# Keys and values of two attention layers by seven products of quarters

## The chip, the cores and the metric

The kernel runs on one core of a Trainium2 chip. Times are device microseconds (us) of one execution; 1428.65 us is the median of three runs of the kernel before. The profile is of one further execution. Its engines are named PE (TensorE, with PEld for its weight loads), DVE (VectorE), ACT (ScalarE), POOL (GpSimd) and SP (SyncE, which issues the DMAs here).

## The reference, cut to what matters

`x` is 8 batches of 512 tokens by 512 features, `ctx` 8 batches of 120 tokens by 512. Four stages follow each other, each added to `x` with a gate:

```python
x = x + tanh(g_xattn[0]) * xattn0(layernorm(x), ctx)          # 16 heads of 32
x = x + tanh(g_ffn[0])   * routed_ffn(layernorm(x))           # 128 experts
x = x + tanh(g_xattn[1]) * xattn1(layernorm(x), ctx, mask)    # with biases and a mask
x = x + tanh(g_ffn[1])   * channel_mix(layernorm(x))

# each xattn:
q, k, v = y @ Wq.T (+ bq), ctx @ Wk.T (+ bk), ctx @ Wv.T (+ bv)
out = softmax(q k^T / sqrt(32)) v @ Wo.T (+ bo)
```

The change concerns `k` and `v` of both attention layers: for each, a 960 x 512 matrix (all tokens of the context) times a 512 x 512 matrix. All of it is float32.

## The kernel before, in words

Both attention layers are objects of one class, `CrossAttention`. Its constructor loads, projects the keys and values and brings the first batches of queries on their way; `run` then goes through 32 tiles of 128 tokens, a slot for each, and `tail` ends the layer. In `run` the slot of tile t computes the scores and softmax of tile t+1, two or fewer products of the queries five tiles ahead, the transposes of the probabilities of t, the output of t-1, and normalizes and transposes later tiles of `x`.

**Keys.** `project_keys` (L333 on) works on two halves of the context, four batches or 480 tokens each. In layer 1 the context comes with tokens on partitions and is first transposed on PE, a batch at a time (`turn_context`); the result `ctxT` is stored to a DRAM tensor, `aside`, at the end. In layer 2 it is loaded from there, already turned. For each of four blocks of 128 features, four matmuls (L345) of 480 columns add up one PSUM bank, and ACT moves it to `kT` with the softmax's scale and, in layer 2, the bias.

**Values.** `project_values` (L379) takes one batch: four matmuls of 512 columns, with the context's 120 tokens as the stationary side, then DVE moves the bank to `v`, adding the bias in layer 2. Three of the eight batches come ahead of the first transposes of `x`, three between them, and two behind the first scores.

**Queries** are already computed by seven products of quarters (`SevenProducts`), as is much of the last stage. Both factors are cut into four quarters of 256 x 256; four sums of quarters of each factor are made first (S1 to S4 of the left, T1 to T4 of the right), each from earlier ones, in the order S3, S1, S2, S4 and T3, T1, T2, T4. Then seven products replace eight. They run in the order p1, p2, p6, p5, p7, p4, p3:

- p1 and p2 need no sum of both sides; p6 needs S2 and T2, p5 S1 and T1, p7 S3 and T3, p4 T4, p3 S4.
- ACT moves p1 and p5 out of PSUM, DVE the others, adding to what is there.
- p7 is followed by two additions in SBUF on POOL (L192, L193): the first reads the quarter that p4's instruction on DVE (L198) changes next, the second changes the quarter that p3's (L203) adds to.

A product of four matmuls takes one of the four PSUM banks tagged `mm`, which are shared by everything in the layer but the scores and half of the probabilities' transposes; these have two tiles of two banks (`s`).

**Order.** In the constructors the order of the instructions on every engine, SP among them, is that of the program text (`manual_schedule(engines=every)`). In `run` of layer 1 only PE's order is by hand, in layer 2 PE's and SP's; a planner orders the rest. All DMAs but two small ones are issued by SP, one after the other.

**Statistics.** `stats(t)` is a pair of DVE instructions for one tile of `x`; after each fourth, POOL makes the batch's scales in four small instructions (L58 to L64). All 32 tiles of both layers have theirs in the constructor.

**Memory.** Pools on the right side of SBUF stack down from its end, and a pool's first tile lies lowest. In layer 2 the pool `at_v` comes first: `ctxT` (15,360 bytes a partition) and `bv` (2,048); below it `at_k` with a second copy of the context, `ctx` (15,360), `wk` and the mask's rows. The keys read `ctx` (L285 loads it in two halves), the values `ctxT` (L302). A tile may be written when the tiles that lay there before have had their last reader. In the routed stage before layer 2 the pool at the end of memory holds `permT` (16,384) and then three small tiles (2,208 with padding); its last readers are the last matmuls of the scatter (L1031). Below lie a pool of the routing, `hT` (16,384) and the experts' weights, which are free some 26 us earlier.

## Time and profile before

| what | us |
|---|---|
| median of three runs (1428.62 to 1429.21) | 1428.65 |
| the profiled execution | 1431.72 |
| its span, first to last instruction | 1429.9 |
| PE busy, in the span | 1383.4 |
| layer 1: first matmul of the keys, of the values | 13.27, 41.69 |
| layer 1: first scores, second scores | 79.33, 91.37 |
| layer 2: first matmul of the keys, of the values | 693.25, 719.1 |
| layer 2: second scores (their mask) | 768.91 |

The mean granted TensorE clock of the profiled execution is 0.995. A row of a timeline gives the start and the length in us, the engine, the line of the kernel and what it writes and reads; `xN` says that N instructions are merged. A row by stretches gives the stretch, its length, and for PE, PEld, DVE, ACT and POOL the busy time and the number of instructions, then the granted clock, the busy share of the DMA engines and GB/s. A row of waits reads "who <- for whom: us in all, times, longest". SPq is SP's queue of DMA issues. A group's mean length of a matmul holds its latency as well; the distance between starts is what a train of them costs.

### The profile page before, as it was taken

The page shows a single profiled execution, that of the slowest core. Times are in us where ns is not written, and L with a number is a line of the kernel's source. Part 1 is how long each engine was busy: PE and PEld are TensorE (multiplying, and loading weights), DVE is VectorE, ACT ScalarE, POOL GpSimd, SP SyncE. Part 2 cuts the span into 40 slices and gives each one's busy share as a digit, 9 for nine tenths or more (in the row PEclk, how much of TensorE's full clock was granted, in tenths as well). Part 3 has the DMA queues.
Part 4 walks back from the last instruction along what each step waited for, and adds up shares of the span by engine and source line. Part 5 has one row for each costly group of instructions (what it writes and reads, how often), then busy time and mean ns, then how long its engine had stood idle before and what let it go on. Part 6 is the DMA issues. An engine that isn't in the chain of part 4 may idle for free.

```text
span 1429.9 us, 32488 instructions
## 1 busy us (share of the span) xinstructions
PE 1383.4 (97%) x13696; PEld 1067.2 (75%) x13696; DVE 1020.5 (71%) x1453; ACT 768.2 (54%) x1870; POOL 644.0 (45%) x576
## 2 busy tenths in 40 slices
PE   7999999999999997999999999999998999999997
PEld 3577777777776787888657777777776788888886
DVE  2666777777777676777566777777777588887786
ACT  1256666666666445444225665666566555445543
POOL 1425545545444000555375575565546333343331
PEclk9999999999999999999999999999999999999999
DMA  9400000000001337432501000000000000000001
GB/s 301 162 9 24 24 23 23 24 23 16 24 31 43 131 125 227 133 106 87 173 0 60 2 2 1 2 2 2 2 30 2 1 30 30 30 30 30 30 16 45
DMA packets 45240, 73.39 MB, mean 51 GB/s; under 512 B 2925, under 2 KB 21869, under 8 KB 44837
## 3 DMA queue, kind: packets, MB, share of 16 engines
q1 hardware_dynamic: 44805, 71.30, 15.0%
q8 instruction: 108, 1.77, 0.5%
q14 instruction: 39, 0.32, 0.1%
q10 hardware_dynamic: 288, 0.00, 0.0%
HBM read 52.55 MB, written 18.74 MB: 50 GB/s over the span
## 4 chain that ended last, share of the span: by engine, by line
PE 72%; DVE 14%; ACT 6%; POOL 4%; issue 3%; DMA 1%; POOLq 0%; SPq 0%; DVEq 0%; ACTq 0%
PE ops L616 15%; PE qps L149 13%; PE tps L564 6%; PE cps L149 5%; PE aps L599 5%; PE s L507 4%; PE kps L345 4%; PE rps L1010 3%; PE vps L379 3%; PE l1ps L925 2%; PE rlps L749 2%; PE ops L1031 2%; PE gps L898 2%; PE xnps L439 2%; DVE rT L990 2%
## 5 line engine op out<-in xcount | busy, mean ns | idle before, releaser
L525 POOL TENSOR_TENSOR pr<-pr,rs 128x960 f32<-128x960 f32 x128 | 229.4, 1795 | 253.2 <-DVE rs L524 231.7
L616 PE MATMUL ops<-wo,aT 128*128 128x512 f32 x512 | 240.6, 596 | 0.7 <-ACT aT L607 0.7
L535 ACT ACTIVATE pr<-s,nmx 128x120 f32<-128x120 f32 x512 | 176.8, 371 | 114.0 <-DVE nmx L532 110.1
L616 PEld LDWEIGHTS ops<-wo,aT 128*128 128x128 f32 x512 | 92.6, 191 | 72.5 <-issue 67.8
L1023 POOL TENSOR_TENSOR r<-r,b 128x1024 f32<-128x1024 f32 x31 | 73.5, 2377 | 145.2 <-ACT r L1022 145.2
L149 PE MATMUL qps<-xnT,wq 128*128 128x256 f32 x512 | 119.6, 381 | 0.0
L564 PEld LDWEIGHTS tps<-ident,pr 128*120 128x120 f32 x864 | 96.7, 138 | 29.6 <-issue 26.2
L543 DVE TENSOR_REDUCE mx<-s 128x8 f32<-128x960 f32 x64 | 74.0, 1156 | 56.6 <-PE s L507 56.6
L535 ACT ACTIVATION_READ_ACCUMULATOR pr<-s,nmx 128x1 f32 x512 | 111.1, 217 | 0.0
L564 PE MATMUL tps<-ident,pr 128*120 128x128 f32 x864 | 104.9, 273 | 2.5 <-ACT pr L535 1.3
L149 PEld LDWEIGHTS qps<-xnT,wq 128*128 128x128 f32 x512 | 95.7, 189 | 15.2 <-issue 1.0
L551 DVE TENSOR_REDUCE sm<-pr 128x8 f32<-128x960 f32 x64 | 73.5, 1148 | 21.9 <-ACT pr L546 21.8
L49 DVE BATCH_NORM_STATS2 bnst<-x 128x6 f32<-128x512 f32 x128 | 86.8, 678 | 1.3
L440 ACT COPY xnT<-xnps 128x512 f32<-128x512 f32 x64 | 38.1, 595 | 82.0 <-PE xnps L439 82.0
L532 DVE TENSOR_REDUCE nmx<-s 128x8 f32<-128x960 f32 x64 | 73.5, 1148 | 8.3 <-PE s L507 8.3
L599 PE MATMUL aps<-prT,v 120*32 120x128 f32 x2048 | 73.3, 278 | 4.1 <-ACT prT L589 2.2
L545 DVE TENSOR_TENSOR pr<-s,mx 128x960 f32<-128x960 f32 x64 | 73.5, 1149 | 0.9
L1276 POOL TENSOR_TENSOR x<-x,cv 128x512 f32<-128x512 f32 x28 | 41.5, 1480 | 70.7 <-DVE cv L1273 70.7
L574 ACT COPY prT<-tps 120x1024 f32<-120x1024 f32 x54 | 55.0, 1019 | 32.7 <-PE tps L564 32.7
L507 PE MATMUL s<-kT,qT 32*128 32x120 f32 x2048 | 71.9, 278 | 0.0
L507 PEld LDWEIGHTS s<-kT,qT 32*128 32x128 f32 x2048 | 66.5, 188 | 6.5 <-issue 6.3
L599 PEld LDWEIGHTS aps<-prT,v 120*32 120x32 f32 x2048 | 53.8, 110 | 18.3 <-issue 8.6
(191 smaller groups left out, 3088.2 us busy)
## 6 DMA issues: line engine op xcount, KB each, us to landing
w<-in_w_dram SPq DMA_DIRECT2D x32, 512.0 KB, 4.8
x<-in_x_dram SPq DMA_DIRECT2D x8, 1024.0 KB, 15.4
aside<-x SPq DMA_DIRECT2D x32, 256.0 KB, 2.0
x<-aside SPq DMA_DIRECT2D x8, 1024.0 KB, 10.5
out_dram<-x SPq DMA_DIRECT2D x14, 512.0 KB, 2.8
wk<-in_wk_dram SPq DMA_DIRECT2D x3, 1024.0 KB, 8.8
wv<-in_wv_dram SPq DMA_DIRECT2D x3, 1024.0 KB, 5.6
wq<-in_wq_dram SPq DMA_DIRECT2D x2, 1024.0 KB, 15.7
```

The lines of the kernel that those rows point to most:

```text
L49: cm.nc.vector.bn_stats(st, cm.x[:, t, :])
L149: self.nc.tensor.matmul(ps[:, m, :], self.a[a][:, k, m * P : (m + 1) * P], self.b[b][:, k, :], start=(k == 0), stop=(k == 1),)
L507: nc.tensor.matmul(s[j // 2][:, j % 2, hc * LK : (hc + 1) * LK], self.qT[b][r : r + 32, hc, toks], self.kT[r : r + 32, hc, keys], start=no ...
L525: nc.gpsimd.tensor_tensor(pr[:, js, :, :], pr[:, js, :, :], rs[:, js, :, :].to_broadcast([P, 2, NC, LK]), ALU.mult,)
L532: nc.vector.tensor_reduce(nmx, sv[1], AX.X, ALU.max, negate=True)
L535: nc.scalar.activation(pr[:, 2 + j, hc, :], sv[1][:, j, hc, :], AF.Exp, bias=nmx[:, j, hc, :], accum_out=sm[:, 2 + j, hc : hc + 1],)
L543: nc.vector.tensor_reduce(mx, sv[0], AX.X, ALU.max)
L545: nc.vector.tensor_tensor(pv, sv[0], mx.to_broadcast([P, 2, NC, LK]), ALU.subtract)
L551: nc.vector.tensor_reduce(sm[:, :2, :], pv, AX.X, ALU.add)
L564: nc.tensor.transpose(ps[:, jj, hc * P : (hc + 1) * P], pr[:, 2 * u + jj, hc, :], self.cm.ident,)
L599: nc.tensor.matmul(aps[32 * j : 32 * j + 32, hc, :], self.v[b // 2][:LK, b % 2, h * HD : (h + 1) * HD], prT[:, j, hc, :], start=True, stop ...
L616: nc.tensor.matmul(ops, self.aT[t][:, c, :], self.wo[:, c, :], start=(c == 0), stop=(c == NC - 1),)
```

## The change

Keys and values are computed with `SevenProducts` too, a half of the context at a time. The left factor is the weight, the right one the half's turned context, 480 tokens in two quarters of 240. The context's sums T1 to T4 of a half are made once, on POOL, and serve keys and values. The sums of `wk` are made on DVE, those of `wv` on POOL. For the values the roles on PE are exchanged (`turned=LK`): a quarter of 120 tokens is the stationary side, 256 columns of `wv` move. Each half gives 7 products of 4 matmuls for keys, of 240 columns, and 7 of 4 for values, of 256.

With it come these edits:

- The context is held in two tiles, `ctxT[0]` and `ctxT[1]`, both in `at_v`; layer 2 loads each of them once, and the second copy is gone. The sums (`csums`), a spare quarter and half a bias (`bvmore`) lie in `at_v` as well, the sums of `wk` in `at_k`, those of `wv` in the second buffer of the probabilities.
- Layer 1 stores the context to `aside` in two halves, after the keys.
- All values are computed before the queries, and the first scores come last in the prologue.
- The statistics of tiles 16 to 31 move into the slots of `run`; those of tiles 8 to 15 stand between the products of the values.
- The softmax's scale is taken by the copies of the transposed `x` (and by `bq`) in place of the keys.
- The queries' T3 lies in the tile of `qT` that they will fill, which is therefore taken one step earlier; the tiles `prT` and `aT` come from a pool that is opened after the prologue.

```diff
 def load(self, ins, loads, mask, biases):
-        self.ctxT = vp.tile([P, NC, B * LK], FP, name="ctxT")
+        half, own = B * LK // 2, 3 if self.turned else 4
+        self.ctxT = [vp.tile([P, NC, half], FP, name=f"ctxT{h}") for h in range(2)]
+        self.csums = [vp.tile([P, own, 2, half // 2], FP, name=f"cs{h}") for h in range(2)]
+        self.q5 = vp.tile([P, 2, 256], FP, name="cq5")
...
+            self.bvmore = vp.tile([LK, D // 2], FP, name="bvmore")
+        wks = kp.tile([P, 3, 2, 256], FP, name="wks")
-        if self.turned:
-            self.ctx = kp.tile([P, NC, B * LK], FP, name="ctx")
...
         def half(h):
             if self.turned:
                 keys = slice(h * B * LK // 2, (h + 1) * B * LK // 2)
-                nc.sync.dma_start(out=self.ctx[:, :, keys], in_=self.aside[:, :, keys])
+                nc.sync.dma_start(out=self.ctxT[h], in_=self.aside[:, :, keys])
...
         weights(self.wv, wvT)
-        if self.turned:
-            nc.sync.dma_start(out=self.ctxT, in_=self.aside)
...
+    def sum_context(self, h, engine):
+        n = B * LK // 4
+        if self.turned:
+            sums = [quarter(self.ctxT[h], 0, 1, n)]
+            sums += [self.csums[h][:, i] for i in range(3)]
+        else:
+            sums = [self.csums[h][:, i] for i in range(4)]
+        for step in SevenProducts.right_steps(self.ctxT[h], *sums, engine, n=n):
+            step()
+        return SevenProducts.right(self.ctxT[h], *sums, n=n)
...
+    def project_keys(self):
+        nc = self.nc
+        self.ctx7 = [None, None]
+        if not self.turned:
+            for b in range(4):
+                self.turn_context(b)
+        self.wk7 = self.sum_weights(self.wk, self.wks, nc.vector)
+        self.ctx7[0] = self.sum_context(0, nc.gpsimd)
+        k = self.keys(0)
+        k.next(2)
+        if not self.turned:
+            for b in range(4, B):
+                self.turn_context(b)
+        k.next(2)
+        self.stats_of_batch(0)
+        self.ctx7[1] = self.sum_context(1, nc.gpsimd)
+        k.next(3)
+        if self.biased:
+            nc.gpsimd.tensor_scalar(self.gbo, self.gbo, self.gate, None, ALU.mult)
+        for t in range(2):
+            self.normalize(t)
...
+        k = self.keys(1)
+        k.next(4)
+        self.stats_of_batch(1)
+        self.wv7 = self.sum_weights(self.wv, [self.wvs[:, i] for i in range(3)], nc.gpsimd)
+        k.next(3)
+        if not self.turned:
+            for h in range(2):
+                keys = slice(h * B * LK // 2, (h + 1) * B * LK // 2)
+                nc.sync.dma_start(out=self.aside[:, :, keys], in_=self.ctxT[h])
 
     def prologue(self):
-        for b in range(3):
-            self.project_values(b)
-        for t in range(2 * TB):
+        nc = self.nc
+        self.sum_query_weights()
+        v = self.values(0)
+        for n in range(7):
+            v.next()
+            if n < 4:
+                self.stats(2 * TB + n)
+        v = self.values(1)
+        for t in range(TB):
+            v.next()
             self.transpose_x(t)
             self.normalize(t + 2)
-            if t < TB - 1:
-                self.project_values(t + 3)
-            elif t < 2 * TB - 1:
-                self.queries(0, t + 1 - TB)
-        rest = self.scores(0)
-        for b in range(B - 2, B):
-            self.project_values(b)
-        rest()
+            self.stats(3 * TB + t)
+        v.next(3)
+        for f in range(NC):
+            self.queries(0, f)
+            self.transpose_x(TB + f)
+            self.normalize(TB + f + 2)
+        self.scores(0)()
...
     def transpose_x(self, t):
-        nc.scalar.copy(self.xnT[b][:, :, i * P : (i + 1) * P], ps)
+        dst = self.xnT[b][:, :, i * P : (i + 1) * P]
+        nc.scalar.activation(dst, ps, AF.Copy, scale=SM_SCALE)
...
     def run(self):
         for t in range(-1, NT - TB - 1):
+            if 4 * TB <= t + 14 < NT:
+                self.stats(t + 14)
```

## The prediction

> **What bounds the kernel now.** I read, in this order: the busy shares of the page, the busy time by stretch, the spacing of the instructions of the two projections and of what the change puts in their place, and the queue of SP with the landings. TensorE first:

> ```profile
> PE 1383.4 (97%) x13696; PEld 1067.2 (75%) x13696; DVE 1020.5 (71%) x1453; ACT 768.2 (54%) x1870; POOL 644.0 (45%) x576
> ```

> By stretch (length, then busy time and instructions of PE, weight loads, DVE, ACT, POOL; granted clock; DMA). The four are keys and the rest up to the first scores in layer 1, then in layer 2:

> ```profile
> 13.30:41.70 28.40, 27.75 (x81) 13.87 (x82) 10.46 (x26) 5.12 (x9) 9.09 (x14) 1.00 1.05 367
> 41.70:93.00 51.30, 50.19 (x239) 31.29 (x238) 35.45 (x68) 18.91 (x41) 15.79 (x27) 1.00 0.19 74
> 693.00:719.00 26.00, 26.00 (x72) 12.26 (x66) 10.59 (x27) 4.63 (x7) 3.58 (x7) 1.00 0.65 229
> 719.00:766.00 47.00, 45.88 (x194) 27.54 (x193) 32.33 (x65) 17.52 (x39) 34.10 (x45) 1.00 0.00 1
> ```

> PE is the bound in all four; nothing else is late by more than 1.1 us. So fewer columns through PE are worth their full time, as long as the other queues keep up. Prices, as the timeline has them (start, length, engine and line):

> ```profile
> 13.27 13.15 PE L345 MATMUL kps<-ctxT,wk 128*128 128x480 f32 x32 [0.65 <-ACT ctxT L371]
> 41.69 10.46 PE L379 MATMUL vps<-wv,ctxT 128*120 128x512 f32 x24
> 64.04 3.62 PE L149 MATMUL qps<-xnT,wq 128*128 128x256 f32 x16
> 33.56 1.27 POOL L88 TENSOR_TENSOR wqs<-wq 128x512 f32<-128x512 f32 x1
> 65.58 0.69 DVE L107 TENSOR_TENSOR xnT<-xnT 128x512 f32<-128x512 f32 x1
> ```

> Every call of matmul stands as two instructions. A long train ends some 0.2 us after its last start, so 32 in 12.9 are 0.403 us each, 24 in 10.3 are 0.429, and 16 in 3.46 are 0.216: in proportion to the columns.

> **The products.** Keys, per layer: 64 x 0.403 = 25.8 us go. In their place come 2 halves x 7 products x 8 instructions of 240 columns; 0.216 x 240/256 = 0.202, so 1.61 a product and 22.6 in all. (From 0.190, the length of a weight load, to 0.216: 1.3 less to 1.6 more.) Values: 64 x 0.429 = 27.5 go, 14 products of 8 x 0.216 = 1.73 come, 24.2. PE has 6.5 us less to do in each layer, 13.1 in both.

> **What comes for it on the other queues.** Per layer POOL gets 8 additions for the sums of the context (128x480), 4 for those of wv, and two after each of four p7. Rows of such additions on POOL run from 1.09 (xns) to 1.59 (kT of the last stage), most at 1.27. I take 1.27 for 512 columns from a weight, 1.27 x 480/512 = 1.2 for the rest: 24 us, in a stretch in which POOL works 9.1 + 15.8 us in layer 1. DVE gets 4 x 0.69 for wk, ahead of need. Each p7, p4 and p3 is now tied to POOL: p4 writes where the first of p7's additions on POOL still reads, and p3 adds to what the second makes. The queries show that wait already:

> ```profile
> DVE qT L198 <- POOL qT L192: 21.4, 16, 1.4
> ```

> There POOL is free when p7 comes. In the change it isn't: in program order p7 of a half stands behind normalization scales and the four sums of the next operand. While p4 and p3 wait, they hold two of the four PSUM banks, and DVE's queue stands still behind p4's instruction, p2 and p6 of the next set among it.

> **Layer 1, queue by queue.** p1 and p2 of the first half need no sums and run from 13.3 to 16.5. The second half of the context landed 15.5 us after its issue at 1.71, so at 17.2: a wait of 0.7 (the old first half hid it). The transposes and the other five products end at 27.1, p1 and p2 of the second half at 30.3. POOL meanwhile: x of batch 0 lands 19.3 us after 3.11, at 22.4; four statistics at 0.80 make 25.6; scales (four small instructions, 1.97) 27.6; three of the context sums 31.2, where p6 gets its operand (1.0 waited); the fourth 32.4, p7's two until 34.7. p5 waits for the bank of p4 (1.5). Keys end at 40.9, before at 41.7. The same again: statistics 40.0, scales 42.1, sums of wv 43.3 to 47.1, p7's two 49.4; p6 of the values waits 1.6 for the third sum and p5 1.4 for a bank. Values end at 70.3 with four transposes of x among them, queries and four more at 85.3, and scores(0) starts at 85.8, when the last addition is in.
> What goes with the order: the old scores(0), at 79.3, had 7.1 us of values behind it while its softmax held the score banks for 5.95 us. Now only 3.9 us (two query products, a transpose) stand there, so scores(1) starts at 85.8 + 6.05 = 91.9, before at 91.4. **Layer 1: +0.5 us**; the 6.5 are gone. With additions at 1.02 and 1.09 it is -0.9, at 1.49 and 1.59 it is +3.0.

> **Layer 2: a load that moves.** The old kernel loads the context twice. SP's queue, and one of its waits (who, for what, us, times, longest):

> ```profile
> 667.29 0.63 SPq L285 DMA_DIRECT2D ctx<-turned  x1
> 667.97 0.61 SPq L291 DMA_DIRECT2D wk<-in_wk_dram  x1
> 668.62 0.53 SPq L285 DMA_DIRECT2D ctx<-turned  x1
> 690.75 0.34 SPq L299 DMA_DIRECT2D bqk<-in_bqk_dram  x1
> 691.21 0.37 SPq L291 DMA_DIRECT2D wv<-in_wv_dram  x1
> 693.31 0.34 SPq L302 DMA_DIRECT2D ctxT<-turned  x1
> ```
> ```profile
> SPq L302 <- PE ops L1031: 1.7, 1, 1.7
> ```

> The keys' copy lay in at_k, over memory that the experts freed at 667. The other lay in at_v, at the end of memory, over permT, which the last scatter of layer 1 reads until 693.3. The change drops the first and keeps only the one in at_v. The tiles there now make 32,000 bytes a partition: ctxT0 lies 24,320 to 32,000 from the end, ctxT1 16,640 to 24,320, and permT 2,208 to 18,592. So ctxT0 still loads at 667, but ctxT1 overlaps permT by 1,952 bytes, waits until 693.3, and bqk, wv and all later loads stand behind it on SP. A half alone lands in

> ```profile
> ctx<-turned SPq DMA_DIRECT2D x1, 960.0 KB, 5.3
> ```

> so at 698.6. bqk, behind it, I put at 699.0 (bv, behind the old ctxT, landed 0.9 after it); were it not held by the data ahead, its own 2.0 us would make 696. Without bqk POOL's first instruction, scale_biases, can't run, and the context's sums are queued behind that. POOL: 699.0 + 0.45 + 3 x 1.2 = 703.1. PE has done p1 and p2 by 696.5 and **waits 6.6 us** for p6. From there as in layer 1, with 1.5 more for a bank; keys end at 724.1 (before 719.1). Then POOL has gbo (1.58), two additions to x (1.26), scales, the wv sums and p7's two until 733.1. Here p1 of the values goes out on DVE too, behind p4 and p3 of the keys, so no bank at all comes free before 732.7: **5.2 us**. Values end at 755.3, scores(0) starts at 770.9, scores(1) at 771 + 6.3 = 777.2; before 768.9. **Layer 2: +8.3** (with bqk at 696, +5.3; additions at the low and high rows, +6.3 and +11.6).

> **What PE does after a gap.** After 9.16 us without work the sixteen transposes of the context took 3.43 us, the next sixteen 1.80, both at a granted clock of 1.00:

> ```profile
> 9.19 3.43 PE L366 MATMUL ctps<-ident,ctx 120*128 120x120 f32 x16 [9.19 <-DMA ctx<-in_ctx_dram]
> 26.25 1.80 PE L366 MATMUL ctps<-ident,ctx 120*128 120x120 f32 x16
> ```

> So 1.6 us are lost behind a gap of 9.2, and none is seen behind one of 2.6 (at 537.6). 6.6 is nearer to the first, 5.2 to the second: I take **+1.6** for the one and 0 for the other (0 to 3.3 in all).
> [...]

> **Edits that I cost at nothing.** Sixteen statistics a layer (0.84 on DVE each, scales on POOL every fourth slot) move from the prologue into the slots of run. DVE waits there for the scores once a slot, which is what hides them:

> ```profile
> DVE mx L543 <- PE s L507: 32.0, 26, 2.2
> ```

> That is 1.2 us each; were the cover gone, up to 13 us a layer, but DVE is busy 224 of 312 us there and PE waits for it next to never, so 0 to +1. The second load of 1,920 KB goes: its reader started at 719, it landed at 703; 0. The store to aside becomes two after the keys; SP has nothing behind it until 87.6, and the reader is layer 2. Scaling moves from the keys to the transposes' copies: ACT took 0.57 with a scale and 0.56 to 0.59 without. T3 goes into the tile of qT one slot earlier; its last reader, scores(t+1), stands ahead on PE. prT and aT start in memory that the values freed one stage earlier.

> **Sum.** -13.1 (PE's work) and +23.5 of new waits and lost cover: 0.5 + 8.3 + 1.6 = +10.4. The profiled execution took 1431.72 us (span 1429.9 and 1.8 around it), so 1442.1; it stood 3.07 above the median of the runs, 1428.65, and against that I say 1439.0.

> **Rivals.** (B) ctxT1 doesn't wait, since memory is laid out otherwise than I add it up. Then bqk lands at 692.8 as before, p6 waits 0.2 instead of 6.6, the gap's price goes: layer 2 +2.2, sum +2.7, 1431.3. For it: my layout is only added up from sizes. Against it: the old ctxT did wait for that scatter. (C) The other side: POOL's queue isn't in the way, because its additions are over before PE comes to them. With them at nothing, layer 1 gives -5.5 and layer 2, which keeps the load's wait, -2.2: 1421. The sign turns where an addition takes about 0.75 us (1.2 gives +8.8, 0.69 gives -1.4, both without the gap's price); the cheapest row is 1.09, which speaks against it. (D) Additions at the dear rows, 1.49 and 1.59: +14.6 without the gap's price, 1443 to 1446. That 240 columns cost no less than 256 would move the sum by 0.2 only, since PE then waits less.

> **How the numbers follow.** My forecast 0.62 (its own range 1434 to 1443), B 0.20 (1428 to 1434), C 0.10 (1418 to 1428), D 0.08. A measurement of this kernel tells 0.2%, 2.9 us, from nothing: 1425.8 to 1431.5 is the same. B lies half in it: faster 0.10, same 0.11, slower 0.79. The range from 1430 to 1445 leaves out C, a third of B and some of D.

> **What would show it.** Right: SP's second load of layer 2 at 693.3, waiting for ops; a PE gap of 6 to 7 us ahead of the third product of the keys, ended by POOL, and one of about 5 in the values; in layer 1 scores(1) within 2 us of 91.4; fewer matmul columns, and a lower busy share of PE. Wrong: that load at 668.6; PE without gaps between 16 and 60; POOL additions far from 1.2; PE waiting on DVE in the slots of run.

## The result, and the profile after

The changed kernel takes 1450.71 us (median, 1449.55 to 1451.50), the kernel before 1428.93 on the same chip: a ratio of 1.0145, 95% interval 1.0125 to 1.0165 (estimated from all runs; it need not be the quotient of the medians). It is 1.45% slower. The forecast was 1439.0, with a range from 1430 to 1445: the sign is right, the loss twice as large as forecast (10.4). The profiled execution took 1450.38 us, its span 1448.6, against 1431.72 and 1429.9 before: +18.7 us to be found in the traces.

The busy line of TensorE and the others after:

```profile
PE 1377.3 (95%) x13888; PEld 1108.0 (76%) x13888; DVE 1040.1 (72%) x1492; ACT 765.3 (53%) x1870; POOL 692.0 (48%) x616
```

TensorE works less, as intended, but only by 6.1 us, and its share falls from 97 to 95%. The same four stretches as in the prediction, keys and the rest up to the early scores of each layer (length, then busy time and instructions of PE, weight loads, DVE, ACT, POOL; granted clock; DMA):

```profile
12.60:45.58 32.98, 27.51 (x130) 24.82 (x129) 16.97 (x31) 5.31 (x9) 17.66 (x19) 0.90 1.05 366
45.58:102.30 56.72, 49.88 (x286) 41.90 (x284) 37.25 (x78) 17.75 (x41) 29.17 (x40) 0.94 0.12 41
701.96:738.49 36.53, 26.82 (x115) 23.88 (x114) 15.30 (x32) 4.25 (x8) 20.94 (x24) 0.86 0.43 141
738.49:786.00 47.51, 43.84 (x246) 37.09 (x245) 27.02 (x50) 12.77 (x21) 33.64 (x32) 1.00 0.13 45
```

Two things are new against the four lines of before. TensorE's busy time is no longer the length: 5.5, 6.8, 9.7 and 3.7 us are idle. And the granted clock, 1.00 in all four before, is 0.90, 0.94 and 0.86 in three of them: part of what counts as busy is work at half speed. The timeline of TensorE has both (start, length, instructions, then in brackets the idle time before and what ended it), up to 85.28 in layer 1, from 712.19 in layer 2:

```profile
34.80 3.56 PE L156 MATMUL kps<-cs,wks 128*128 128x240 f32 x8 [4.02 <-DVE kT L198]
38.16 2.72 PE L156 MATMUL kps<-cs,wk 128*128 128x240 f32 x8
40.72 1.78 PE L156 MATMUL kps<-cs,wks 128*128 128x240 f32 x8
...
51.46 1.99 PE L156 MATMUL vps<-wvs,cs 128*120 128x256 f32 x8 [2.26 <-DVE kT L198]
53.28 1.89 PE L156 MATMUL vps<-wv,cs 128*120 128x256 f32 x8
...
81.73 3.75 PE L156 MATMUL qps<-xnT,wqs 128*128 128x256 f32 x8 [3.66 <-DVE mv L50]
85.28 3.16 PE L156 MATMUL qps<-xnT,wq 128*128 128x256 f32 x8
...
712.19 3.57 PE L156 MATMUL kps<-cs,wks 128*128 128x240 f32 x8 [6.72 <-POOL cs L107]
...
728.60 2.67 PE L156 MATMUL kps<-cs,wks 128*128 128x240 f32 x8 [2.99 <-DVE kT L198]
731.07 2.72 PE L156 MATMUL kps<-ctxT,wk 128*128 128x240 f32 x8
```

The waits stand at the third product of a set (p6), in both layers; one of 1.45 for the context's second half and small ones at the scores come to them. Behind each wait of 2.99 us or more, the next products take up to 3.6 us from start to start instead of 1.62 or 1.73 (38.16 less 34.80, 40.72 less 38.16, 85.28 less 81.73); behind the wait of 2.26 they don't. (At 81.73 the row names a statistic, L50; the sums of the queries, L107, run in the same queue at 80.88 and 81.67.) What the wait at 34.80 hangs on is a row of VectorE, p4's addition, which itself waited for POOL:

```profile
34.09 0.66 DVE L198 TENSOR_TENSOR kT<-kT,kps 128x480 f32<-128x480 f32 x1 [7.59 <-POOL kT L192]
```

And SP's queue in layer 2, where the prediction had the late load, with POOL's first instruction there:

```profile
675.98 0.60 SPq L285 DMA_DIRECT2D ctxT<-turned  x1
...
702.07 0.56 SPq L285 DMA_DIRECT2D ctxT<-turned  x1
702.74 0.56 SPq L299 DMA_DIRECT2D bqk<-in_bqk_dram  x1
```
```profile
707.92 0.23 POOL L320 TENSOR_SCALAR bqk<-bqk 128x4 f32<-128x4 f32 x1 [7.93 <-DMA bqk<-in_bqk_dram]
```

The second half of the context and, behind it, bqk go out only when the last scatter is through, as forecast. The account, by three marks on TensorE (scores(1) of layer 1; the first product of layer 2; scores(1) of layer 2): layer 1 is 9.67 us longer (91.37 to 101.04), layer 2 11.30 (75.66 to 86.96), run and the routed stage between them 0.96 shorter, and all behind 1.3 shorter. Together 18.7. The ratio of all runs makes it 20.7: the profiled execution of the kernel before stood 3.07 above its median, and it has three windows of 3.41 us at half speed outside the four stretches (at 545.4 and 1084.7), where this execution of the changed kernel has none.

### The profile page after: what moved, and what is told of

It is laid out like the page before. It is cut to its first block, busy times and chain, and to the rows that moved or that the text cites. A ratio compares the mean times of both kernels' runs of the same rounds, so it can differ in the third digit from the quotient of the medians.

```text
span 1448.6 us, 33007 instructions
## 1 busy us (share of the span) xinstructions
PE 1377.3 (95%) x13888; PEld 1108.0 (76%) x13888; DVE 1040.1 (72%) x1492; ACT 765.3 (53%) x1870; POOL 692.0 (48%) x616
## 3 DMA queue, kind: packets, MB, share of 16 engines
q1 hardware_dynamic: 45573, 69.34, 14.6%
## 4 chain that ended last, share of the span: by engine, by line
PE 67%; DVE 15%; ACT 6%; POOL 6%; issue 3%; DMA 2%; SPq 0%; POOLq 0%; ACTq 0%; DVEq 0%
PE ops L698 14%; PE qps L156 12%; PE tps L646 6%; PE cps L156 6%; PE aps L681 4%; PE s L589 4%; PE rps L1094 3%; PE vps L156 2%; PE rlps L833 2%; PE l1ps L1009 2%; PE ops L1115 2%; PE xnps L519 2%; DVE rT L1074 2%; PE gps L982 2%; ACT pr L617 2%
## 5 line engine op out<-in xcount | busy, mean ns | idle before, releaser
L646 PEld LDWEIGHTS tps<-ident,pr 128*120 128x120 f32 x864 | 96.8, 138 | 31.2 <-issue 25.9
L156 PE MATMUL qps<-xnT,wqs 128*128 128x256 f32 x256 | 65.3, 399 | 4.8 <-DVE mv L50 3.7
L521 ACT ACTIVATE xnT<-xnps 128x512 f32<-128x512 f32 x64 | 38.8, 607 | 56.5 <-PE xnps L519 56.5
## 6 DMA issues: line engine op xcount, KB each, us to landing
x<-aside SPq DMA_DIRECT2D x8, 1024.0 KB, 10.4
```

What stands on the lines that cost most here:

```text
L156: self.nc.tensor.matmul(ps[:, m, :], rows[:, k, m * n : (m + 1) * n], columns[:, k, :], start=(k == 0), stop=(k == 1),)
L646: nc.tensor.transpose(ps[:, jj, hc * P : (hc + 1) * P], pr[:, 2 * u + jj, hc, :], self.cm.ident,)
```

## The experiments

Four causes can be read from the trace, and it can't tell how they share the loss: **the clock** behind each wait; **bqk** behind the late load; **the statistics**, which in layer 1 stand not in run's slots but between 72 and 94 us, ahead of the queries' sums on VectorE; and **the bank** of p4, held until POOL has come to p7's additions (the waits that L198 ended). The medians of the kernel before differ by up to 0.3% from one set of runs to another (1428.93 to 1433.07), so every kernel is compared with the kernel before of its own set:

| kernel | before, us | this, us | ratio | 95% interval |
|---|---|---|---|---|
| changed kernel | 1428.93 | 1450.71 | 1.0145 | 1.0125 to 1.0165 |
| e1_fill: waits filled with dead products | 1433.07 | 1449.74 | 1.0121 | 1.0101 to 1.0141 |
| e2_bqk: bqk loaded earlier | 1433.07 | 1445.90 | 1.0090 | 1.0071 to 1.0108 |
| e3_pin: statistics held in run | 1433.07 | 1448.11 | 1.0106 | 1.0091 to 1.0121 |
| e4_dve: p7's additions on VectorE | 1430.64 | 1433.45 | 1.0023 | 1.0007 to 1.0040 |
| c2: bqk, statistics, sums first | 1430.64 | 1424.16 | 0.9963 | 0.9949 to 0.9976 |
| c1: the same, and p7 on VectorE | 1430.64 | 1422.52 | 0.9952 | 0.9934 to 0.9969 |
| c3: the same, and two more edits | 1431.50 | 1418.33 | 0.9918 | 0.9897 to 0.9939 |
| changed kernel, in c3's set | 1431.50 | 1451.80 | 1.0151 | 1.0128 to 1.0174 |

### The clock in place: the waits filled

```diff
+    def fill(self, n, w, x):
+        ps = self.p_s.tile([P, 2, 512], FP, name="s", tag="s")[:, :, : B * LK // 4]
+        for _ in range(n):
+            for m in range(2):
+                for k in range(2):
+                    self.nc.tensor.matmul(ps[:, m, :], w[:, k, m * P : (m + 1) * P],
+                                          x[:, k, :], start=(k == 0), stop=(k == 1))
...
         k = self.keys(1)
-        k.next(4)
+        k.next(2)
+        self.fill(1 if self.turned else 2, self.wk7["A11"], self.ctx7[0]["B11"])
+        k.next(2)
```

and likewise at the other places.

> Nothing of the change is undone. Products whose result nobody reads (each eight instructions of 240 columns, 1.61 us) are put into TensorE's waits of the changed kernel, in PSUM that the scores don't use yet: in layer 1 two ahead of the third product of the keys' second half (wait of 4.02 us), one ahead of the third of the first values (2.26), two ahead of the third query product (3.66); in layer 2 four (6.72), one (2.99) and one (2.25) at the same places of keys and values. Each ends before its wait ends, so that the wait itself is still paid; only TensorE is not idle for so long. Theory 1 (what the prediction sized wrongly is the clock: after an idle stretch of some 3 us the next two products run at half speed): the granted clock stays at 1.00 over 25 to 102 and 702 to 790 us, the products after the waits take 1.62 and 1.73 instead of 2.5 to 3.5, and of the 9.4 us that the trace of the changed kernel shows lost so (2.7 + 3.1 + 1.9 + 1.8) between 7.5 and 9.5 come back, since the sums that end the later waits hang partly on the first product: 1441.2 to 1443.2 us. Rival (those products are slow because of what they read or because of POOL's use of memory beside them, and the waits alone make the loss): they stay slow, 1449.5 to 1452 us.

Measured: 1.0121, some 0.24% (3.4 us) below the changed kernel, less than the 7.5 to 9.5 expected; the two intervals overlap, so the time alone doesn't show a gain. The products themselves did what the theory of the clock says. TensorE's timeline of this kernel (L438 is a dead product) and its stretches:

```profile
30.29 3.40 PE L438 MATMUL s<-ctxT,wk 128*128 128x240 f32 x16
34.51 1.89 PE L156 MATMUL kps<-cs,wks 128*128 128x240 f32 x8 [0.82 <-DVE kT L198]
...
97.61 1.27 PE L607 MATMUL s<-kT,qT 32*128 32x120 f32 x32 [1.60 <-ACT pr L635]
98.81 3.24 PE L156 MATMUL qps<-xnT,wqs 128*128 128x256 f32 x8
```
```profile
25.20:97.00 71.80, 67.44 (x358) 58.39 (x357) 42.38 (x91) 18.39 (x40) 40.26 (x54) 1.00 0.39 142
97.00:103.60 6.60, 5.99 (x46) 5.03 (x47) 6.35 (x10) 4.24 (x15) 3.58 (x2) 0.74 0.01 2
703.00:790.00 87.00, 80.92 (x456) 70.78 (x457) 46.38 (x87) 21.90 (x50) 55.99 (x57) 1.00 0.26 84
```

Nothing of the change's work was altered, the wait of the keys' second half ends at 34.51 (34.80 in the changed kernel), and the product behind it takes 1.72 from start to start (34.51 to 36.23) instead of 3.36. So the slow products were the clock's, not those of operands or memory. But scores(1) of layer 1 comes only 3.4 us earlier (97.61) and that of layer 2, counted from the layer's first product, 1.9 (85.1). What is won ahead of a wait that POOL's queue ends is in part lost in that wait: the first values start 2.87 earlier in layer 1, their third product only 1.95. And behind the wait of 1.60 at scores(1) a new half-speed window stands (0.74 from 97.0 to 103.6), which costs some 1.7. The mean granted clock of the profiled execution is 0.996 (0.990 in the changed kernel), and it is 1.0 shorter in all. The 9.5 us of slow products are a real price, but not one that comes back alone while POOL's queue ends the waits.

### The clock by itself

> No part of the computation of the reference is in this kernel, and its output isn't the reference's: trains of 40 matmuls of 128x240 (80 instructions, some 16.1 us at the full clock) on TensorE, and between them chains of 4 to 24 small additions on VectorE (about 0.3 us each) that read the last product and make the operand of the next train, so that TensorE is idle for known times of about 1.5 to 8 us, 24 of them, most lengths twice and in mixed order. Theory 1 (an idle stretch over a threshold halves the clock for some microseconds, whatever its length beyond that): trains after up to 2.3 us take 16.1, those after 3 us and more some 1.8 to 3.1 us longer, about the same after 3 as after 8, with a granted clock of 0.5 at their start. Rival, as the prediction sized it from the kernel before (a gap of 9 costs 1.6, one of 2.6 nothing, those between by their length): next to nothing up to 5, about 1 at 6 to 8. Second rival (what decides is where the gap falls in a fixed raster of time): the same length costs once and not the other time.

An addition of a chain took 0.41 us (L38, 408 ns). A train of 80 instructions at the full clock is an estimated 16.4 us (80 x 0.2025, from the 1.62 us between products of eight such instructions in the changed kernel, and 0.2 at the end). Some of the trains, in the order of the program:

```profile
41.14 16.47 PE L17 MATMUL ps<-y,w 128*128 128x240 f32 x80 [1.83 <-DVE y L38]
59.87 18.16 PE L17 MATMUL ps<-y,w 128*128 128x240 f32 x80 [2.27 <-DVE y L38]
...
102.05 17.92 PE L17 MATMUL ps<-y,w 128*128 128x240 f32 x80 [3.15 <-DVE y L38]
...
146.71 19.47 PE L17 MATMUL ps<-y,w 128*128 128x240 f32 x80 [4.04 <-DVE y L38]
...
323.88 17.94 PE L17 MATMUL ps<-y,w 128*128 128x240 f32 x80 [4.04 <-DVE y L38]
344.97 19.32 PE L17 MATMUL ps<-y,w 128*128 128x240 f32 x80 [3.15 <-DVE y L38]
```

The one gap of 1.83 costs 0.1; every gap from 2.27 up to 10.7 costs 1.5 to 3.1, with no order by length. 4.04 costs 3.1 at one place and 1.6 at another, 3.15 costs 1.6 and 3.0, 6.26 costs 1.9. So the threshold of 3 that the first theory gave is wrong, and sizing a gap by its length, as the prediction did, is wrong. Of the second rival the fixed raster of time holds, but not its wording: no gap of 2.27 or more was free here, and what changes between two gaps of one length is whether one window is lost or two. Windows of 3.41 us laid on the changes of the granted clock show it, here around the gaps of 2.27 and 4.04:

```profile
57.24:60.65 3.41, 1.14 (x6) 0.74 (x5) 2.04 (x5) 0.00 (x0) 1.00 0.00 0
60.65:64.06 3.41, 3.41 (x10) 2.90 (x9) 0.00 (x0) 0.00 (x0) 0.50 0.00 0
64.06:67.47 3.41, 3.41 (x18) 3.17 (x17) 0.00 (x0) 0.00 (x0) 1.00 0.00 0
...
142.58:145.99 3.41, 0.08 (x1) 0.00 (x0) 3.05 (x8) 0.00 (x0) 1.00 0.00 0
145.99:149.40 3.41, 2.69 (x7) 2.32 (x8) 0.63 (x2) 0.00 (x0) 0.50 0.00 0
149.40:152.81 3.41, 3.41 (x10) 2.90 (x9) 0.00 (x0) 0.00 (x0) 0.50 0.00 0
```

(After the length: busy time and instructions of PE, of weight loads, DVE, POOL; granted clock.) Behind the windows with 1.14 and 0.08 us of work, a third or less, stands one at 0.50. The clock came back behind a window with 3.41 us of work: for the shorter gap one window is lost, for the longer one two, the first of them with 2.69. The two places of the fence lie 25 windows of 3.41 us apart (60.65 and 145.99). The half-speed stretches of the changed kernel's profile start 14, 198 and 204 windows behind the first (33.22, 81.01, 709.06, 729.54), those of the kernel before 158 apart (545.39, 1084.70), each one or two windows long but for one at the very end of each profile: one raster from the first to the last in each of these executions. Where it lies differs from run to run: in the second profile of the changed kernel the first half-speed window starts at 33.95. Counted over the windows of the profiles of the kernel before and the changed kernel, from 12.7 us to the end: the seven full-speed windows with a busy share of 0.39 or less, two of them at the very end, were all followed by half speed; of the five from 0.48 to 0.54 one was (0.48); above that none was. The changed kernel's wait of 4.02 and the wait of 3.36 at the same product of layer 2 in the kernel with bqk ahead, in two fences, show how a long wait can be free:

```profile
29.81:33.22 3.41, 0.97 (x5) 0.57 (x3) 0.00 (x0) 0.20 (x1) 3.25 (x4) 1.00 1.05 388
33.22:36.63 3.41, 1.83 (x5) 1.57 (x6) 1.87 (x3) 0.00 (x0) 2.00 (x2) 0.50 1.05 387
36.63:40.05 3.42, 3.42 (x10) 2.88 (x9) 1.61 (x4) 0.00 (x0) 0.00 (x0) 0.50 1.05 386
40.05:43.46 3.41, 3.41 (x18) 3.20 (x18) 2.76 (x7) 0.56 (x1) 1.03 (x2) 1.00 1.05 389
```
```profile
714.80:718.21 3.41, 1.60 (x8) 1.15 (x7) 0.00 (x0) 0.81 (x2) 3.25 (x4) 1.00 0.43 165
718.21:721.63 3.42, 1.88 (x9) 1.78 (x10) 2.08 (x4) 0.00 (x0) 3.42 (x3) 1.00 0.00 0
```

The first fence is the changed kernel (ACT's column comes in before POOL's, DMA at the end), the second the other. There the 3.36 us fell half into one window and half into the next (1.60 and 1.88 busy, shares of 0.47 and 0.55), and the clock stayed at 1.00.

### bqk ahead of the late load

```diff
         weights(self.wk, wkT)
-        half(1)
         if self.biased:
             ...
             nc.sync.dma_start(out=self.bqk, in_=bqk_in)
+        half(1)
```

> The load of bqk is issued ahead of the load of the second half of the context instead of behind it; all else is the changed kernel. Theory (the prediction's step on layer 2: the wait of 6.7 us ahead of the third product of the keys comes from bqk, which stands on SP behind a load that waits for the last scatter, since POOL's first instruction needs bqk and the context sums stand behind it): bqk is issued at some 691, once its own memory is free as in the kernel before, and lands before 694; POOL starts its sums at about 702, when the tiles of the sums come free of the last scatter, the third ends at 705.7, and the wait falls from 6.72 to about 0.5. With it go the 1.9 us of slow products behind it: -8.1, 1441.5 to 1444 us. The second half of the context still lands at 707 and the waits of the second half of the keys (3.0) and of the values (2.25) stay. Rival (the sums wait for memory that the scatter frees, or for the data, and not for bqk): 1449.5 to 1452 us with the wait where it was.

Measured: 1.0090, 0.55% or 7.9 us below the changed kernel, in the range expected (in the profiles layer 2 is 5.9 shorter to scores(1)). bqk was issued at 697.09, ahead of the layer's first product at 699.59, and the wait of 6.72 became 1.73, not 0.5. It ends with VectorE's sums of wk now. VectorE and then POOL of this kernel:

```profile
700.32 1.14 DVE L88 TENSOR_TENSOR wks<-wk 128x512 f32<-128x512 f32 x1
701.50 1.58 DVE L88 TENSOR_TENSOR wk<-wk 128x512 f32<-128x512 f32 x1
```
```profile
699.70 1.22 POOL L107 TENSOR_TENSOR cs<-ctxT 128x480 f32<-128x480 f32 x1 [0.38 <-PE ops L1115]
700.99 1.53 POOL L107 TENSOR_TENSOR ctxT<-ctxT 128x480 f32<-128x480 f32 x1
```

The wait behind the keys' second half stayed (3.36), that of the values grew to 3.34, with slow products behind it (the first takes 3.24 from start to start, 734.92 to 738.16, instead of 1.73). In layer 2 of the changed kernel, where POOL still waited for bqk, the same four additions of wk took 0.68 to 0.69 each. Side by side with POOL's they take up to 1.58, and POOL's 1.53 instead of 1.20. (Layer 1 of the changed kernel has the same: the first two of wk take 0.68 and 0.69, the two beside POOL's 1.57; there TensorE doesn't wait for them.) Both slow down. In turn a pair of additions would take 1.89 (0.69 and 1.20, an estimate from the times alone); side by side one of each comes every 1.6. So "4 x 0.69 for wk, ahead of need" held in layer 2 only as long as bqk kept POOL away.

### The statistics held in run

```diff
-                self.stats(t + 14)
+                self.stats(t + 14, self.tc.keep_in_program_order)
```

(each bn_stats is queued behind what stands ahead of it on VectorE).

> The sixteen statistics that the change moves into the slots of run are held there: each is pinned behind the work that stands ahead of it in program order on VectorE, so that the planner can't pull it forward in layer 1. All else is the changed kernel. Theory (in layer 1 the planner moves all sixteen to 72 to 95 us, ahead of the sums that the queries wait for, which makes the wait of 3.66 us at the third query product and the 3.1 us of slow products behind it): the wait falls to the 1.1 us that the kernel before has, the products behind it take 1.73, scores(1) starts 5.7 us earlier, 95.3 instead of 101.0, and the slots pay nothing, since VectorE waits for the scores there: 1444 to 1446.5 us. Rival (the statistics are dear wherever they stand: in the slots TensorE then waits on VectorE, 0.84 us each): scores(1) comes earlier by 5.7, but the slots grow by up to 13, 1448 to 1458 us. Second rival (the wait comes from the normalization scales or POOL): nothing moves, 1449.5 to 1452.

Measured: 1.0106, 0.39% or 5.6 us below the changed kernel. The queries' third product in layer 1:

```profile
78.01 1.97 PE L158 MATMUL qps<-xnT,wqs 128*128 128x256 f32 x8 [1.11 <-DVE xnT L109]
```

3.66 became 1.11, the value of the kernel before, the product behind it starts 1.80 later, and scores(1) comes at 94.29 instead of 101.04. From scores(1) to the first product of layer 2 it takes 601.66 us (94.29 to 695.95), in the changed kernel 600.92: the slots of run take the sixteen statistics for at most 0.7. The first rival, that they are dear wherever they stand, falls.

### p7's additions on VectorE

```diff
             lambda: self.q5[:, :, :n],
-            bias=self.bias(1),
+            bias=self.bias(1), engine=self.nc.vector,
```

and the same in values().

> The two additions behind each p7 of keys and values run on VectorE instead of POOL; all else is the changed kernel. Theory (the waits of 4.0 and 3.0 us ahead of the third product of the keys' second half and of 2.3 us in the values come from p4, which holds its PSUM bank until the first of these additions is through on POOL, and that stands behind scales and four sums): both waits on VectorE's kT fall under 0.5 us; in their place TensorE waits for the sums themselves, about 0.9 us in layer 1's keys and 0.5 to 1 in the values; the slow products behind the two waits of the keys (2.7 and 1.8 us) take 1.62 again. Layer 1 -7.7 us, layer 2 -6.0, VectorE's own queue gives back 0 to 1.5: against the kernel before, which the changed one exceeds by 1.45%, a rest of +0.4 to +0.8%. The wait of 6.7 us in layer 2 and that of 3.7 us in layer 1's queries stay. Rival (no bank is short; the third product waits for the sums of the second operand): the waits stay within 1 us, now ended by POOL: +1.2 to +1.5%.

Measured: 1.0023, 1.2% or 17 us below the changed kernel; expected were some 14. TensorE at the three places in layer 1 and at the keys' second half in layer 2, where it no longer waits at all:

```profile
31.59 1.89 PE L156 MATMUL kps<-cs,wks 128*128 128x240 f32 x8 [1.25 <-POOL cs L107]
...
43.61 1.99 PE L156 MATMUL vps<-wvs,cs 128*120 128x256 f32 x8 [0.20 <-POOL wvs L88]
...
71.61 1.97 PE L156 MATMUL qps<-xnT,wqs 128*128 128x256 f32 x8 [1.38 <-POOL nmr L63]
...
713.43 1.78 PE L156 MATMUL kps<-cs,wks 128*128 128x240 f32 x8
```

In the keys and the values the releaser is POOL's sums now, not p4's addition: it was the bank. This one edit takes away most of the loss, and more than forecast because the queries' wait went too (3.66 to 1.38), although the statistics still stood ahead of the queries' sums. In the changed kernel p4's addition of the second values waits on VectorE for POOL (2.06 us, until 75.77), and the statistics, the queries' sums and p2 are queued behind it. That wait and the statistics each needed the other to hold up the queries; taking away either is enough.

### All causes at once

c1 combines the three edits with one more: the sums come ahead of the statistics whose scales stood ahead of them on POOL. c2 is the same without p7's additions on VectorE.

```diff
-        self.stats_of_batch(0)
         self.ctx7[1] = self.sum_context(1, nc.gpsimd)
+        self.stats_of_batch(0)
...
-        self.stats_of_batch(1)
         self.wv7 = self.sum_weights(...)
+        self.stats_of_batch(1)
```

> Four edits at once, all arithmetic of the change kept: bqk loaded ahead of the context's second half; run's statistics pinned in their slots; p7's two additions on VectorE; the sums of the context's second half and of wv stand ahead of the statistics (so of POOL's scales) of batches 0 and 1. If the causes are the four that the trace of the changed kernel names, layer 1 loses the waits of 4.0 and 2.3, keeps 1.1 of the 3.7, and loses 5.8 of slow products, and layer 2 loses 5.0 of 6.7, 3.0, 2.25 and 3.7 of slow products; what is left is the 13.1 us that TensorE has less to do, less some 4 us of small waits (0.7 for the context's second half, 1.7 for the sums of wk, 1.1 in each layer's queries and 0.9 at scores(1)): 6 to 9 us below the kernel before, -0.4 to -0.6%. If the moved statistics or seven products with their VectorE work cost something that the waits hid (the other 1,300 us), it is not below: -0.2 to +0.3%.

> As the kernel with four edits, but p7's additions stay on POOL: bqk ahead, statistics pinned, sums ahead of the scales. Theory (what holds p4's bank is the queue ahead of p7's additions on POOL, and that the sums now run before): in layer 1 the sums of the second half end at 25 instead of 33, p7's additions run behind POOL's scales, about 27 to 30, and p4 gives its bank back by 31.0, so that the third product of the second half waits under 0.5 us; in layer 2 the second half lands at 705, the sums end at 710 and p7's additions follow scales and sums at about 713 to 715, a wait of 0 to 1; in the values much the same. Then 0.2 us or so behind the other: -0.2 to -0.6% against the kernel before. Rival (POOL's additions themselves, two of 1.2 us behind p7 with VectorE standing still until then, are enough to hold a bank too long): waits of 1 to 2.5 us stay at each half, six or seven of them, some with slow products behind: +0.1 to +0.6%.

Measured: 0.9952 and 0.9963. Both are faster than the kernel before, as expected, and not to be told from each other. In c1 what TensorE still waits for up to scores(1) is 0.9 for the context's second half in layer 1, 1.73 for the sums of wk in layer 2, and in each layer 1.1 in the queries and 0.9 or 0.8 at the scores. Layer 1 reaches scores(1) at 85.70 (before 91.37), layer 2 needs 72.11 to its own (before 75.66). The profiled execution of c1, the fastest of nine, has a mean granted clock of 0.999, the others go down to 0.993; by that figure at most some 4 of its 1418.8 us are at half speed (an estimate). Where p7's additions run matters little once the sums are out of their way; in c2 one wait of 1.0 in the values of layer 2 is left. Its rival, waits of 1 to 2.5 at every half, falls.

The gains of e2, e3 and e4 add up to 31 us, c1 with one edit more has 27.6: they overlap, as the queries' wait shows.

c3 adds two edits for what c1 still waits for:

```diff
+            order="1256743",      # keys: p5 ahead of p6
...
-        v.next(3)
+        v.next()
         for f in range(NC):
             self.queries(0, f)
             ...
+            if f == 0:
+                v.next()
-        self.scores(0)()
+        rest = self.scores(0)
+        v.next()
+        rest()
```

> The kernel with four edits and two more. In the keys p5 goes ahead of p6, since S1 and T1 are made before S2 and T2: of the 1.73 us that TensorE waits in layer 2 for the sums of wk about 0.1 is left. The last two products of the second values move behind the first two query products and behind scores(0), where TensorE waits 1.1 us for the queries' sum and 0.9 for the softmax that holds the score banks, in each layer. Theory (these waits are in TensorE's own way and the products fill them): 1.6 + 2 x 2.0, some 5.5 us less than the kernel with four edits, -0.7 to -1.0% against the kernel before. Rival (the values' last products push VectorE's work in front of the queries' or the softmax's, and the waits only move): within 0.15% of the kernel with four edits, -0.35 to -0.6%.

Measured: 0.9918, 11.7 us below the kernel before; the rival, that the waits only move, falls, if narrowly (its range ended at -0.6%, the interval ends at -0.61%). Two of the four stretches of this kernel, the keys of layer 2 and the rest up to scores(1):

```profile
684.25:707.38 23.13, 23.02 (x114) 21.22 (x113) 19.34 (x34) 4.14 (x8) 21.85 (x19) 1.00 0.66 222
707.38:752.52 45.14, 45.14 (x257) 38.69 (x257) 32.47 (x57) 16.54 (x39) 27.09 (x28) 1.00 0.14 48
```

TensorE is busy all the time again in these two, at the full clock, and layer 2 takes 68.27 us to scores(1): 7.4 less than before, of which 6.5 are the work that seven products save. Behind scores(1) of layer 2 a part does move: the wait of the first transposes of the probabilities for VectorE, 0.45 before and 1.47 in the changed kernel and c1, is 2.31 in c3, with slow transposes behind it (eight take 1.96 us from 761.48, 1.09 at the same place in the changed kernel). The changed kernel on the same chip:

> The changed kernel as it is, on the chip of the kernel with six edits, so that the two can be compared on one chip: +1.3 to +1.6% against the kernel before, and the same seven half-speed stretches of the clock within two.

Measured: 1.0151, so that c3 is 2.3% below it. Seven windows of 3.41 us stand at half speed, as in the first profile (mean granted clock 0.990 in both), but not the same seven: the wait of 4.16 in the keys of layer 1 costs one instead of two, the products come earlier, the wait in the first values, which POOL's queue ends, grows from 2.26 to 3.19, and the window lost less is lost there.

## Why the prediction was right and wrong

**The products: right.** Keys in the changed kernel stand 1.62 us apart and values 1.73, against 1.61 and 1.73; the saving of 6.5 us a layer is what c3 shows in layer 2 (7.4 shorter to scores(1)).

**The late load of layer 2: right**, in all its steps. The load of the context's second half was issued at 702.07 behind the last scatter, POOL's first instruction waited for bqk until 5.96 after the layer's first product (5.75 forecast), and TensorE's wait was 6.72 (6.6). Rival B, that the load doesn't wait, falls with SP's row.

**POOL's additions: right in price** (mostly 1.19 to 1.21 for 480 columns, 1.26 to 1.27 for 512; 1.2 and 1.27 were taken), which rules out rival D. Rival C, that they aren't in the way, was false of the change; it is what the later kernels make true.

**The banks: mechanism right, place and size off.** "p5 waits for the bank of p4 (1.5)" took the bank that came free first. In the trace the wait that p4's addition (L198) ends stands at p6, four products behind p4: the four banks go round in turn, and both waits became one. (ACT had emptied p1's bank at 30.01, and p6 still waited from 30.78 to 34.80.) In layer 1 it is 4.02 for the keys (1.0 + 1.5 forecast) and 2.26 for the values (1.6 + 1.4), in layer 2 2.99 (1.5) and, with a wait of 0.31 behind it, 2.56 (5.2). In that last place the bank came free even later than forecast, 42.4 us after the layer's first product (39.5: "no bank at all comes free before 732.7"), but TensorE came to it 5.8 later, by the longer wait ahead of it and the slow products, and so had less left to wait. The sum is 11.8 where 12.2 were forecast; that they agree is luck.

**"Edits that I cost at nothing": wrong for the statistics.** "DVE waits there for the scores once a slot, which is what hides them" is true of the slots, and e3_pin shows it. But in layer 1 they never went there: only TensorE's order is written out in run, and the planner put sixteen ready statistics ahead of the queries' sums. With the wait for POOL on VectorE that made 3.66 instead of 1.11, and slow products behind it: 5.6 us in all.

**The clock: the step that failed most.** "6.6 is nearer to the first, 5.2 to the second: I take +1.6 for the one and 0 for the other" was sized from two gaps of before and put the waits of layer 1 at nothing. The first of the two, at 9.19, stands at a granted clock of 1.00 in the record, so it isn't shown to be the same effect. The trace has 2.7 + 3.1 in layer 1 and 1.9 + 1.8 in layer 2, 9.5 us of slow products at a granted clock of 0.50, where 1.6 were forecast. The gap of 2.99 cost as much as that of 6.72 (1.8 and 1.9). The evidence was in the trace of before, eight microseconds behind the gap that the prediction used. There a window that TensorE filled by 1.63 of 3.41, cut up by small waits, is followed by one at half speed:

```profile
541.98:545.39 3.41, 1.63 (x52) 1.43 (x52) 2.76 (x3) 2.23 (x3) 0.00 (x0) 1.00 0.21 81
545.39:548.80 3.41, 3.41 (x74) 3.41 (x68) 0.49 (x1) 0.00 (x0) 0.00 (x0) 0.50 0.02 5
```

The account by terms, forecast and measured: layer 1, -6.5 work, waits 6.2 and 7.7, the queries' longer wait 0 and 2.55, clock 0 and 5.8. That makes 9.6 of the 9.67 measured. (Left out are 1.3 of waits that only the kernel before has and, against them, a wait of 0.92 at scores(1); the forecast had 0.8 of lost cover there.) Layer 2: -6.5 work, waits 13.3 and 12.3, clock 1.6 and 3.7; what is left, 1.5 forecast as lost cover of the scores and 1.8 measured, of which a wait of 0.80 at scores(1) is on record. That is 11.3. The 2.3 us that the rest of the kernel takes less were not forecast. The kernel before has half-speed stretches there, of one window at 545.4 and of two at 1084.7, some 5 us lost, and the changed one has none; against that, TensorE is idle for 1.7 longer behind scores(1) of layer 2 (15.8 and 14.0), above all for VectorE at the first transposes. No run was made to separate this.

## What to carry over

Price a wait of the engine that sets the time twice: its length, and what its clock does behind it; in the changed kernel every wait that left a window of 3.41 us 0.28 busy or less cost another 1.8 to 3.1, among the trains every gap from 2.27 up another 1.5 to 3.1, and in the kernel before a window of 0.48, cut up by shorter waits, was followed by half speed too. When a change ties a PSUM bank's release to a second engine, follow that engine's queue up to the releasing instruction and count the banks in turn, and expect what is won ahead of such a wait to be lost in it. Work that is moved into a stretch which a planner orders is moved only once it is pinned there.
